# Loading scan operands earlier, computing the decay two units ahead, and wider queue reach in the ordering clock of a four-layer kernel

## The chip, the cores and the metric

The kernel runs on one core of a Trainium2 chip. The metric is the device time of one execution in microseconds (us), lower is better. The engines are TensorE (PE; its weight loads are PEld), VectorE (DVE), ScalarE (ACT) and GpSimd (POOL). SyncE (SP) issues DMAs; so do ACT and POOL.

## The reference

Four images of 96 x 64 x 64 pass a state-space scan (layer 0), a deformable convolution (layer 1), a Fourier layer with a feed-forward (2) and an attention with a feed-forward (3). The part that matters here is the scan, in four directions, 192 channels and 16 states:

```python
def step(h, inp):
    d_t, u_t, b_t, c_t = inp
    dA = jnp.exp(d_t[..., None] * A)
    h = dA * h + (d_t * u_t)[..., None] * b_t[:, :, None, :]
    y = jnp.einsum('bkdn,bkn->bkd', h, c_t)
    return (h, y)
...
_, ys = lax.scan(step, h0, (dl, ul, bl, cl))
```

## The kernel before

The scan is cut into 1536 *units* of 128 partitions (16 states x 8 channels) by 1024 pixels. Eight units make a *block* (64 channels), 24 a *step*. A unit runs: load `da` (ACT issues the DMA), `exp` on ACT, spread of `du` into PSUM on PE, multiply and scan on DVE, multiply by C on POOL, sum over states on PE, and once a block an eviction (`settle`) on ACT. The loop issues these stages skewed:

```python
for n in range(len(units) + 7):
    ...                                       # waits until layer 0 has made what unit n+4 needs
    for stage, m in ((self.inflow, n + 1), (self.decay, n + 1)):
        if at(m) is not None:
            stage(at(m))
    if n % 2 == 1 and at(n - 5) is not None:
        self.total(at(n - 5), at(n - 4))
    if loaded < len(units):
        self.fetch(units[loaded], units[loaded - 1])      # da of n+4; at a step start also bc,
        loaded += 1                                       # at a block start also du
    for stage, m in ((self.recur, n), (self.weigh, n - 2)):
        if at(m) is not None:
            stage(at(m))
    ...                                       # settle, store
    clock.unit(self.scanned[1])
    yield True                                # other layers' work is issued here
```

```python
def decay(self, u):                           # ACT
    u.decayed = self.net.clock.add(ACT, 1.15, 0.0)
    a = u.k * (DI // D8) + u.n
    self.net.nc.scalar.activation(u.da, u.da, AF.Exp, scale=self.al[:, a : a + 1])

def inflow(self, u):                          # PE, into one of two PSUM buffers
    u.spread = self.net.clock.add(PE, 1.1, self.scanned[1])
    db = self.ps.tile([128, 2, CH], F32, name=f"db{u.key}", tag="db", bufs=2)
    for h in range(2):
        self.net.nc.tensor.matmul(db[:, h, :], lhsT=self.rep[:96, u.s % 4, :],
            rhs=u.du[u.s // 4][:, h * CH : (h + 1) * CH], start=True, stop=True)
    ...
def recur(self, u):                           # DVE
    nc, clock = self.net.nc, self.net.clock
    clock.add(DVE, 1.22, u.spread)
    self.scanned = (self.scanned[1], clock.add(DVE, 2.33, u.decayed))
    nc.vector.tensor_mul(u.db, u.db, u.bc[:, 0, :])
    u.hh = self.sp.tile([128, T], F32, name=f"hh{u.key}", tag="hh", bufs=6)
    ...
    nc.vector.tensor_tensor_scan(u.along(u.hh), u.along(u.da), u.along(u.db), first, ALU.mult, ALU.add)
```

All other work is issued between units by two streams: `ends` (layer 0's inputs, then layers 2 and 3 image by image) and `middle` (layer 0's output, layer 1). In the traces an engine runs its instructions in the order in which they are issued (the change and fetch_late below, whose loads differ in time, show one and the same sequence of PE's 32696, DVE's 4484, ACT's 5798 and POOL's 4755 instructions), so the order is decided while the program is built, by a model *clock* that adds up estimated costs. It admits a step of work only if no engine that it uses is modelled further ahead of DVE than its *reach*:

```python
AHEAD = (2.0, 1.5, 3.0, 4.0)                  # reach of PE, DVE, ACT, POOL in us
PACE = 4.9
...
def has_room(self, work, ready):
    now = self.now()                          # max(ends[DVE], due); due grows by PACE a unit
    ...
    return all(not w or e <= now + a for w, e, a in zip(work, self.ends, AHEAD))
```

So AHEAD and the `clock.add` calls cost nothing on the chip; they only move instructions.

## Time and profile before

| | us |
|---|---|
| median of 3 runs | 9585 |
| first to last scan unit | 7799, that is 5.08 a unit |
| last scan unit to the end of layer 1's last sampling | 687 |
| rest of the third image | 245 |
| fourth image | 482 |

The stretches are read off the trace. The last three are called the *tail*. The chain of work that ended last is the view that says where the end came from (shares of the span, by engine and by line); before:

```profile
PE 29%; POOL 23%; DMA 16%; DVE 15%; issue 9%; ACT 6%; ACTq 1%; SPq 0%; DVEq 0%; POOLq 0%
POOL hh L904 11%; POOL g L1225 7%; DVE hh L895 7%; DMA da<-de 5%; PE pc L659 4%; DVE db L892 3%; PE ps L1248 3%; PE f L1339 3%; PE py L922 2%; PE po L1125 2%; PE db L879 2%; DMA du<-du 2%; DMA g<-table,idx 1%; ACT da L873 1%; POOL lw L747 1%
```

No engine carries a third of it, and loads carry 16%. Two groups of the page (count, then busy us and mean ns, then idle time of the engine just before them and what ended most of it):

```profile
L895 DVE TENSOR_TENSOR_SCAN hh<-da,st,db 128x1024 f32<-128x1024 f32 x1152 | 2703.1, 2346 | 494.9 <-ACT da L873 294.7
L873 ACT ACTIVATE da<-da,w_al 128x1024 f32<-128x1024 f32 x1536 | 1736.9, 1146 | 808.1 <-DMA da<-de 479.6
```

DVE waits before the scan, for the exp; ACT waits before the exp, for the load of `da`. It is tempting to read this as one cause. The experiments show that it is two.

### The profile page before, as it was taken

What the parts mean: (1) busy time and instruction counts of PE and PEld (TensorE: products, weight loads), DVE (VectorE), ACT (ScalarE), POOL (GpSimd) and SP (SyncE); (2) the same over time, 40 slices, a digit from 0 to 9 for tenths busy, and PEclk for the clock granted to TensorE, in tenths of its full rate; (3) what the DMA queues carried; (4) which work ended last, traced back from release to release, by engine and by line L of the source; (5) the groups of instructions that cost most, each with busy time, mean ns of one, the idle gap of its engine ahead of it and who ended that gap; (6) DMA issues with size and microseconds to landing.
All of it is one profiled execution on the core that took longest, in us unless ns stands there. A gap on an engine that the chain in (4) does not pass through costs nothing.

```text
span 9574.8 us, 93668 instructions
## 1 busy us (share of the span) xinstructions
PE 7024.3 (73%) x32684; PEld 3207.5 (33%) x32696; DVE 6758.3 (71%) x4516; ACT 4184.1 (44%) x5766; POOL 6460.4 (67%) x4755
## 2 busy tenths in 40 slices
PE   6675866696767667877666777777667787878887
PEld 2111311131222333212223444223334542377474
DVE  0378777877787888778877888888888789333313
ACT  3674666555544433555444233443333345311323
POOL 0585578666789998677899885667989657276101
PEclk9676977697877778877777888777778787889888
DMA  1476677766777877777777786767778777344010
GB/s 48 130 199 163 177 190 192 184 181 175 199 199 203 212 201 195 189 199 200 204 208 203 188 213 170 179 160 195 188 194 209 175 186 171 75 145 134 19 58 16
DMA packets 775821, 1609.55 MB, mean 168 GB/s; under 512 B 247665, under 2 KB 338829, under 8 KB 773238
## 3 DMA queue, kind: packets, MB, share of 16 engines
q10 hardware_dynamic: 300672, 985.79, 40.9%
q1 hardware_dynamic: 400950, 391.20, 15.0%
q0 software_dynamic: 73728, 226.57, 8.8%
q8 instruction: 260, 4.26, 0.2%
q14 instruction: 211, 1.73, 0.1%
HBM read 1346.94 MB, written 256.29 MB: 167 GB/s over the span
## 4 chain that ended last, share of the span: by engine, by line
PE 29%; POOL 23%; DMA 16%; DVE 15%; issue 9%; ACT 6%; ACTq 1%; SPq 0%; DVEq 0%; POOLq 0%
POOL hh L904 11%; POOL g L1225 7%; DVE hh L895 7%; DMA da<-de 5%; PE pc L659 4%; DVE db L892 3%; PE ps L1248 3%; PE f L1339 3%; PE py L922 2%; PE po L1125 2%; PE db L879 2%; DMA du<-du 2%; DMA g<-table,idx 1%; ACT da L873 1%; POOL lw L747 1%
## 5 line engine op out<-in xcount | busy, mean ns | idle before, releaser
L904 POOL TENSOR_TENSOR hh<-hh,bc 128x1024 f32<-128x1024 f32 x1536 | 3655.7, 2382 | 344.7 <-DVE hh L895 240.8
L895 DVE TENSOR_TENSOR_SCAN hh<-da,st,db 128x1024 f32<-128x1024 f32 x1152 | 2703.1, 2346 | 494.9 <-ACT da L873 294.7
L892 DVE TENSOR_TENSOR db<-db,bc 128x1024 f32<-128x1024 f32 x1536 | 1866.5, 1215 | 365.3 <-PE db L879 363.1
L873 ACT ACTIVATE da<-da,w_al 128x1024 f32<-128x1024 f32 x1536 | 1736.9, 1146 | 808.1 <-DMA da<-de 479.6
L879 PE MATMUL db<-du,rep 96*128 96x512 bf16 x3072 | 1120.5, 454 | 975.3 <-DVE hh L895 848.3
L1225 POOL DMA_INDIRECT g<-table,idx x1152 | 1429.9, 1241 | 397.8 <-issue 225.0
L922 PE MATMUL py<-hh,w_fold 128*32 128x512 f32 x6144 | 1153.0, 770 | 107.5 <-POOL hh L904 73.1
L895 DVE TENSOR_TENSOR_SCAN hh<-da,db 128x1024 f32<-128x1024 f32 x384 | 878.2, 2287 | 184.2 <-ACT da L873 131.1
L1248 PE MATMUL ps<-w_ident,g 128*96 128x128 f32 x4608 | 719.1, 321 | 365.8 <-DVE g L1234 159.3
L879 PEld LDWEIGHTS <-rep 96*128 96x128 bf16 x3072 | 275.0, 105 | 2036.8 <-issue 1250.7
L1234 DVE TENSOR_TENSOR g<-g,wt 128x3456 f32<-128x3456 f32 x128 | 544.6, 4255 | 408.1 <-DMA g<-table,idx 385.1
L1248 PEld LDWEIGHTS ps<-w_ident,g 128*96 128x96 f32 x4608 | 625.9, 151 | 560.3 <-issue 211.6
L902 POOL COPY st<-hh 128x1 f32<-128x1 f32 x1152 | 276.7, 240 | 793.0 <-DVE hh L895 753.6
L1256 ACT COPY st<-ps 96x384 f32<-96x384 f32 x384 | 182.5, 477 | 1245.5 <-PE ps L1248 1167.0
L746 POOL TENSOR_TENSOR w<-w,ex 128x512 f32<-128x512 f32 x192 | 246.9, 1286 | 565.2 <-ACT w L743 546.2
L659 PE MATMUL pc<-pad,wc 96*128 96x512 f32 x1152 | 545.1, 621 | 62.3 <-DMA wc<-wc_d 50.7
L1485 POOL CAST xqf<-fl 96x512 fp8e5<-96x512 f32 x64 | 55.0, 864 | 652.7 <-DVE fl L1443 617.8
L749 DVE SCALAR_TENSOR_TENSOR rl<-pd,lw 128x512 f32<-128x512 f32 x192 | 129.9, 677 | 397.1 <-POOL lw L747 396.0
L922 PEld LDWEIGHTS py<-hh,w_fold 128*32 128x32 f32 x6144 | 167.7, 123 | 676.0 <-issue 396.8
L768 PE MATMUL pr<-ex,w_ident 128*128 128x512 f32 x384 | 288.9, 843 | 83.7 <-POOL ex L758 39.4
L659 PEld LDWEIGHTS pc<-pad,wc 96*128 96x128 f32 x1152 | 223.4, 198 | 357.4 <-issue 328.3
L1426 DVE TENSOR_TENSOR t<-t,o 96x512 f32<-96x512 f32 x64 | 81.3, 1270 | 313.5 <-PE o L1424 313.4
(247 smaller groups left out, 9660.6 us busy)
## 6 DMA issues: line engine op xcount, KB each, us to landing
da<-de ACTq DMA_DIRECT2D x1536, 512.0 KB
du<-du ACTq DMA_DIRECT2D x384, 192.0 KB
bc<-bcd ACTq DMA_DIRECT2D x128, 512.0 KB
du<-du SPq DMA_DIRECT2D x128, 384.0 KB
y<-yb SPq DMA_DIRECT2D x384, 128.0 KB
de<-rl SPq DMA_DIRECT2D x128, 256.0 KB
m<-in_dft SPq DMA_DIRECT2D x128, 256.0 KB
du<-du SPq DMA_DIRECT2D x128, 192.0 KB
```

Source lines behind the costliest of these rows:

```text
L659: nc.tensor.matmul(pp, lhsT=wc[:, q, g * 128 : (g + 1) * 128], rhs=pad[:, r0 + dy : r0 + dy + NR, dx : dx + W], start=(q == 0), stop=(q == 8),
L768: nc.tensor.matmul(pr, lhsT=net.ident, rhs=ex, start=True, stop=False)
L873: self.net.nc.scalar.activation(u.da, u.da, AF.Exp, scale=self.al[:, a : a + 1])
L879: self.net.nc.tensor.matmul(db[:, h, :], lhsT=self.rep[:96, u.s % 4, :], rhs=u.du[u.s // 4][:, h * CH : (h + 1) * CH], start=True, stop=True,)
L892: nc.vector.tensor_mul(u.db, u.db, u.bc[:, 0, :])
L895: nc.vector.tensor_tensor_scan(u.along(u.hh), u.along(u.da), u.along(u.db), first, ALU.mult, ALU.add)
L904: self.net.nc.gpsimd.tensor_mul(u.hh, u.hh, u.bc[:, 1, :])
L922: nc.tensor.matmul(py[p0 : p0 + 32], lhsT=self.fold[:, u.i, :], rhs=hc[:, h * CH : (h + 1) * CH], start=u.sums["add"] is None and u.i == 0 ...
L1225: nc.gpsimd.indirect_dma_start(out=g[:, k, :], out_offset=None, in_=self.tables[b % 2], in_offset=bass.IndirectOffsetOnAxis(ap=idx[:, 9 * ...
L1234: nc.vector.tensor_mul(g4, g4, w4.unsqueeze(2).to_broadcast([128, 36, C]))
L1248: nc.tensor.matmul(pt[:, k, :], lhsT=g[:, k0 + k, c * C : (c + 1) * C], rhs=net.ident, is_transpose=True, start=(c == 0), stop=(c == 3),)
L1339: nc.tensor.matmul(pt[64 * part : 64 * part + 64, c, :], lhsT=d[:, :, c0 + c], rhs=matrix[:, 64 * part : 64 * part + 64], start=True, stop ...
```

## The change

It loads `bc` in the middle of the step before and `du` in the block before; takes the exp two units ahead of its scan (six `da` buffers, five loads ahead); gives the model clock longer reaches; and lets the clock know that a scan needs a free `hh` buffer and that a block's first sum needs the last one evicted. A narrower weight and shared tags make room in SBUF.

```diff
-AHEAD = (2.0, 1.5, 3.0, 4.0)
+AHEAD = (3.0, 3.0, 5.0, 7.0)
...
-        ahead = 4
+        ahead = 5
...
                 self.decay(at(0))
+                self.decay(at(1))
                 self.inflow(at(0))
-            for stage, m in ((self.inflow, n + 1), (self.decay, n + 1)):
+            for period, tick, load in ((24, 12, self.fetch_step), (8, 2, self.fetch_block)):
+                u = at(n - n % period + period)
+                if n % period == tick and u is not None and made(u):
+                    load(u)
+            for stage, m in ((self.inflow, n + 1), (self.decay, n + 2)):
...
+            if at(n) is not None:
+                self.recur(at(n), at(n - 6).summed if n >= 6 else 0.0)
...
-        u.da = sp.tile([128, T], F32, name=f"da{u.key}", tag="da", bufs=5)
+        u.da = sp.tile([128, T], F32, name=f"da{u.key}", tag="da", bufs=6)
...
-        self.scanned = (self.scanned[1], clock.add(DVE, 2.33, u.decayed))
+        self.scanned = (self.scanned[1], clock.add(DVE, 2.33, max(u.decayed, free)))
...
-        self.net.clock.add(PE, 1.5 + 1.3 * (u.i == 0), max(u.weighed, v.weighed))
+        ready = max(u.weighed, v.weighed, self.settled if u.i == 0 else 0.0)
+        u.summed = v.summed = self.net.clock.add(PE, 1.5 + 1.3 * (u.i == 0), ready)
...
-        self.net.clock.add(ACT, 0.6, 0.0)
+        self.settled = self.net.clock.add(ACT, 0.6, u.summed)
```

Cut: the split of `fetch` into three functions, the narrower weight, and the tags.

More of the change, by code (lines that the diff above doesn't have):

```diff
@@ L111, in prepare @@
     om = np.concatenate([ow[0::2], ow[1::2], w["L1_conv_mask_w"].reshape(9, C, 9)])
-    a["wom"] = wide(om.transpose(1, 2, 0))
+    a["wom"] = wide(om.transpose(1, 2, 0), 96)
     ob = w["L1_conv_offset_b"]
@@ L503, in __init__ @@
         self.ts = slice(self.j * T, (self.j + 1) * T)
+        self.bc = self.du = None
     def along(self, t):
@@ L558, in __init__ @@
         self.scanned = (0.0, 0.0)
+        self.settled = 0.0
     def before(self, b):
@@ L800, in at, with made @@
             return units[m] if 0 <= m < len(units) else None
+        def made(u):
+            return all(
+                (u.b, u.k, both, 2 * u.j + h) in self.ready for both in (False, True) for h in range(2)
+            )
         for n in range(len(units) + 7):
             for m in range(loaded, min(n + ahead + 1, len(units))):
-                u = units[m]
-                while not all(
-                    (u.b, u.k, both, 2 * u.j + h) in self.ready for both in (False, True) for h in range(2)
-                ):
+                while not made(units[m]):
                     yield False
@@ L822, in scan @@
                 loaded += 1
-            for stage, m in ((self.recur, n), (self.weigh, n - 2)):
-                if at(m) is not None:
-                    stage(at(m))
+            if at(n) is not None:
+                self.recur(at(n), at(n - 6).summed if n >= 6 else 0.0)
+            if at(n - 2) is not None:
+                self.weigh(at(n - 2))
             if n % 2 == 0 and at(n - 6) is not None and at(n - 6).i == 3:
@@ L839, in fetch @@
         halves = [slice(j * T + h * CH, j * T + (h + 1) * CH) for h in range(2)]
-        if u.first_of_step:
-            u.bc = sp.tile([128, 2, T], F32, name=f"bc{u.key}", tag="bc")
-            for s in range(2):
-                src = self.bc_d[b][k][NS * s : NS * s + NS, ts]
-                nc.scalar.dma_start(u.bc[:, s, :], src.unsqueeze(1).to_broadcast([NS, D8, T]))
-            if u.step == 0:
-                u.state = sp.tile([128, DI // D8], F32, name=f"st{u.key}", tag="st")
-            else:
-                u.state = before.state
-        else:
-            u.bc, u.state = before.bc, before.state
-        if u.first_of_block:
-            u.du = []
-            for q in range(2):
-                t = sp.tile([96, T], BF16, name=f"du{u.key}_{q}", tag=f"du{q}")
-                nc.scalar.dma_start(t, self.du_d[b][k][:, c0 + 32 * q : c0 + 32 * q + 32, ts])
-                u.du.append(t)
+        if not u.first_of_step:
+            u.bc = before.bc
+        elif u.bc is None:
+            self.fetch_step(u)
+        if u.first_of_step and u.step == 0:
+            u.state = sp.tile([128, DI // D8], F32, name=f"st{u.key}", tag="st")
+        else:
+            u.state = before.state
+        if not u.first_of_block:
+            u.du, u.sums = before.du, before.sums
+        else:
             u.sums = {"add": None}
-        else:
-            u.du, u.sums = before.du, before.sums
+            if u.du is None:
+                self.fetch_block(u)
         if u.i == 1 and u.s == 1 and (k == 0 or u.back):
@@ L865, in fetch, with fetch_step, fetch_block @@
         self.net.clock.add(ACT, 0.6, self.scanned[1])
-        u.da = sp.tile([128, T], F32, name=f"da{u.key}", tag="da", bufs=5)
+        u.da = sp.tile([128, T], F32, name=f"da{u.key}", tag="da", bufs=6)
         src = self.de_d[b][k][c0 + D8 * u.s : c0 + D8 * u.s + D8, ts]
         nc.scalar.dma_start(u.da, src.unsqueeze(0).to_broadcast([NS, D8, T]))
+    def fetch_step(self, u):
+        u.bc = self.sp.tile([128, 2, T], F32, name=f"bc{u.key}", tag="bc")
+        for s in range(2):
+            src = self.bc_d[u.b][u.k][NS * s : NS * s + NS, u.ts]
+            self.net.nc.scalar.dma_start(u.bc[:, s, :], src.unsqueeze(1).to_broadcast([NS, D8, T]))
+    def fetch_block(self, u):
+        u.du = []
+        for q in range(2):
+            t = self.sp.tile([96, T], BF16, name=f"du{u.key}_{q}", tag=f"du{q}")
+            c0 = 64 * u.g + 32 * q
+            self.net.nc.scalar.dma_start(t, self.du_d[u.b][u.k][:, c0 : c0 + 32, u.ts])
+            u.du.append(t)
     def decay(self, u):
@@ L886, in inflow, with recur @@
         u.db = db.rearrange("p h t -> p (h t)")
-    def recur(self, u):
+    def recur(self, u, free):
         nc, clock = self.net.nc, self.net.clock
         clock.add(DVE, 1.22, u.spread)
-        self.scanned = (self.scanned[1], clock.add(DVE, 2.33, u.decayed))
+        self.scanned = (self.scanned[1], clock.add(DVE, 2.33, max(u.decayed, free)))
         nc.vector.tensor_mul(u.db, u.db, u.bc[:, 0, :])
@@ L1015, in gated @@
                     cs = slice(j * CH, (j + 1) * CH)
-                    za = op.tile([128, CH], F32, name=f"za{b}_{j}", tag="za")
+                    za = op.tile([128, CH], F32, name=f"za{b}_{j}", tag="ya")
                     nc.sync.dma_start(za, self.z_d[b][:128, cs])
-                    zc = op.tile([D2, CH], F32, name=f"zc{b}_{j}", tag="zc")
+                    zc = op.tile([D2, CH], F32, name=f"zc{b}_{j}", tag="yc")
                     nc.sync.dma_start(zc, self.z_d[b][128:, cs])
@@ L1121, in chunk @@
                 r0 = j * NR
-                po = net.mm(f"po{b}_{j}")
+                po = net.mm(f"po{b}_{j}", 96)
                 for k in range(9):
```

## The prediction

> **What bounds the kernel now.** I read the page's busy shares first, then the busy time by stretch, then VectorE's (DVE) and ScalarE's (ACT) waits inside the long stretch, then the chain of work.
>
> The page's first part of the kernel before:
>
> ```profile
> PE 7024.3 (73%) x32684; PEld 3207.5 (33%) x32696; DVE 6758.3 (71%) x4516; ACT 4184.1 (44%) x5766; POOL 6460.4 (67%) x4755
> ```
>
> No engine is full on average. The busy time by stretch (columns: stretch, length, busy us and count of each engine, granted clock, DMA share, GB/s), cut where the 1536 units of the scan begin and end and where the last image's deformable layer and the third image end:
>
> ```profile
> 361.00:8161.00 7800.00, 5648.51 (x24317) 2310.58 (x24328) 6284.79 (x3946) 3641.66 (x4814) 5931.96 (x4325) 0.79 0.74 190
> 8174.00:8847.00 673.00, 549.55 (x3744) 409.58 (x3746) 224.70 (x203) 144.10 (x277) 402.52 (x325) 0.89 0.44 121
> 8847.00:9095.00 248.00, 201.38 (x1088) 117.35 (x1086) 92.60 (x128) 95.58 (x193) 43.25 (x34) 0.90 0.09 26
> 9095.00:9575.00 480.00, 391.21 (x3028) 276.96 (x3028) 131.35 (x189) 138.65 (x270) 41.59 (x34) 0.85 0.13 37
> ```
>
> Row one is the scan: 7800 us, 5.08 us a unit, and DVE, its nearest engine to a bound, is busy 6285 of them (81%). The other rows are a tail of 1414 us in which TensorE (PE) is busy 82% and no scan is left to hide anything. What DVE waits for in the scan:
>
> ```profile
> DVE hh L895 <- ACT da L873: 425.8, 212, 9.9
> DVE db L892 <- PE db L879: 363.1, 179, 16.4
> DVE g L1234 <- DMA g<-table,idx: 149.9, 44, 8.7
> DVE rl L749 <- POOL lw L747: 124.3, 54, 12.6
> DVE hh L895 <- PE py L922: 82.4, 61, 13.4
> ```
>
> (us in total, times, longest). 1 is the decay exp coming late from ACT, 2 the spread of du into PSUM late from PE, 5 an hh buffer not yet summed. What makes ACT late:
>
> ```profile
> ACT st L1256 <- PE ps L1248: 826.9, 241, 17.2
> ACT da L873 <- DMA da<-de: 479.6, 169, 16.6
> ...
> ACT yb L933 <- DMA du<-du: 123.9, 57, 20.6
> ```
>
> ACT runs in order, so an eviction waiting for PE holds the exp behind it, and a late load holds all. The chain through the second image's sampling (2780 to 3780 us) is another regime:
>
> ```profile
> by line: POOL hh L904 31.8%; POOL g L1225 25.0%; issue 8.9%; DMA g<-table,idx 4.3%; DVE hh L895 3.4%; POOL lw L747 3.1%; POOL w L746 2.8%; POOL st L902 2.6%; PE ps L1248 2.6%; DVE g L1234 2.4%; POOL ex L758 1.8%; DMA du<-du 1.7%; DVE db L89
> ```
>
> There GpSimd (POOL) carries the chain (92 to 94% busy in the trace, some 5.3 us a unit).
>
> **What the Trainium skill says.** "Perfetto Trace Analysis", Optimization Strategy, says that a kernel can have several regimes, that interleaving them may help, and to look for the gaps on the engine of interest and their semaphores. The trace agrees: three regimes (DVE starved, POOL-bound sampling, PE tail). "DMA: Bandwidth & Descriptors", Issuing engines are not separate DMA queues, says DMAs of all issuers share the same 16 engines and interleave; its Anatomy section gives a fit of 2 us plus bytes over 436 GB/s, so 3.2 us (an estimate) for a lone 512 KB da. Here pieces of 13 to 18 us of "DMA da" and "DMA du" stand in the chain, at a DMA share of 0.74: loads do not run alone, and bunching costs. The same section says DMA engines do not wait on semaphores, the issuing sequencer does; here that is ACT, and each issue takes it 0.53 us (da), 0.58 (bc), 0.74 (du).
>
> **The change part by part.**
>
> (1) Fetch of bc and du away from the step and block starts. Before, at a step start ACT issued 2 bc, 2 du and one da in a row, 2x0.58+2x0.74+0.53 = 3.2 us, and the da queued behind 1.4 MB. Grouping DVE's idle time before the two scan instructions by a unit's place in its step of 24 (from the trace) gives 124 us at place 0, 39 at 1, 66 at 14, 70 at 8, 47 at 16, 81 at 22, 59 at 23, and about 28 at an ordinary place. The excess over 28 at those seven is 290 us. The settle copy behind a du issue (the 123.9 us row) and the hh waits at places 14 and 22 belong to it. The issues are the same in number; I take 60% of it as removed: 175 us.
>
> (2) Decay two units ahead, sixth da buffer, loads five ahead. A load still has three units before its exp, so no DMA slack is won; the exp gains one more unit (5 us) before its scan. Of the 426 us, some 218 lie at the places counted in (1); of the other 208 (mean wait 2.0 us, longest 9.9) two thirds go: 140 us.
>
> Sum 315 us. But 555 of the 1536 units pass during sampling, where POOL sets the pace and DVE's saving is not time: 64% counts, 200 us.
>
> (3) Queue reach (2, 1.5, 3, 4) to (3, 3, 5, 7). This moves instructions, none are added. In the program order, by scan unit: sampling of images 0, 1, 2 takes 187, 165, 141 units against 197, 191, 167, so POOL's shared stretch is denser, 62 units fewer at 5.3 us and more at 4.9: some 25 to 50 us, I take 40. Image 1's last feed-forward, wholly in the tail before, ends inside the scan, and image 2's norm, first hidden layer and first DFT too. In the trace before that is 8174 to 8535, 360 us of the tail.
>
> The tail does not shrink by that. Image 3 must pass its deformable layer, which stands in the tail in both orders. Beside it PE gets about the same load from the other stream (summing that stream's matmul times, some 660 us before and 675 after), so its 673 us stay. But when it ends, image 2 has left only part of its attention and the last feed-forward (some 80 us of the trace's 9012 to 9095), against 248. The tail gets 248 - 80 = 165 us shorter; image 3's 480 us stay.
>
> What it costs: some 45 us of DVE work go into the scan, half of it into idle time (+25), and fuller PE queues ahead of the spread matmuls, which are still only one unit ahead, make the PE db wait grow by a tenth (+35).
>
> (4) The ordering clock now knows of hh buffers and settling; 96 columns for one weight and shared za/ya tags only make room in SBUF. No time of their own.
>
> **Sum:** scan -200 - 40 + 60 = -180; tail -165; together -345 from 9585: 9240 us, 3.6% faster.
>
> **Rivals.** (a) The PE spread becomes the wait. Two PSUM buffers tie it to the scan two units back, PE's reach grows by half, and the row is already 363 us. If it doubles, the scan gains nothing and only the tail's 165 us stay: about 9420, "same". Against it: PE is 72% busy in the scan, and the clock counts PE's delay before it admits more.
> (b) POOL queues seven us ahead hold the weighting back, hh buffers run out, and "hh <- PE py" grows from 82 us to several hundred in sampling: 9350 to 9450. Against it: the clock now waits for the hh buffer in its model, and sampling is POOL-bound already.
> (c) DMA becomes the bound: 0.74 share now, 0.78 at a scan 5% shorter, and da lands no earlier relative to its exp. Then decay two ahead is hidden anyway, and (2) is worth half: 9290.
> (d) It all lands: all 315 us count and denser sampling brings more; 9060 or lower.
>
> **Range and chances.** (d) and (a) set the range, 9060 to 9430. The 2% mark is 9394, 155 us above my number, close to where the scan gives nothing. I give 0.82 to faster, 0.15 to same, 0.03 to slower; slower needs both (a) and (b) at large size, with the tail gain surely there in the order.
>
> **What will show it right or wrong.** Step (1): the excess at places 0, 8, 22 and 23 and the row "yb <- DMA du" fall below half. Step (2): "hh <- ACT da" falls from 426 to under 150 us. Step (3): from the last scan to the end some 1250 us; image 2 ends about 80 us after the last sampling; sampling stretches busier than 94% on POOL. Costs: "db <- PE db" near 400 us. Scan near 7620 us, 4.96 a unit. The prediction is wrong if DVE's waits merely change name (DVE busy share in the scan stays 81%), or if the last deformable layer takes longer than 673 us because image 2 now competes harder.

## The result, and the profile after

The changed kernel took 9300 us (median of 4 runs, 9284 to 9337) against 9588 for the kernel before on the same chip (4 runs, 9584 to 9614): ratio 0.970, 95% interval 0.9666 to 0.9733. All runs were fast. A ratio here is the mean time of one kernel's fast runs over that of the other's fast runs of the same rounds, so not quite the ratio of the medians quoted.

The chain of work that ended last, after:

```profile
PE 28%; POOL 27%; DVE 17%; DMA 12%; issue 9%; ACT 6%; SPq 1%; ACTq 1%; DVEq 0%; another core or an unknown queue 0%; POOLq 0%
POOL hh L927 12%; POOL g L1249 9%; DVE hh L918 8%; PE pc L662 4%; DVE db L915 4%; PE py L946 3%; PE ps L1272 2%; PE f L1363 2%; PE db L901 2%; POOL lw L750 2%; POOL st L925 1%; DMA da<-de 1%; POOL w L749 1%; PE pd L1286 1%; PE po L1149 1%
```

Loads fell from 16% to 12% of the chain, `da` from 5% to 1%, and POOL and DVE took their place. The same two groups of the page, and the multiply's, after:

```profile
L918 DVE TENSOR_TENSOR_SCAN hh<-da,st,db 128x1024 f32<-128x1024 f32 x1152 | 2703.6, 2347 | 240.2 <-PE py L946 77.3
L895 ACT ACTIVATE da<-da,w_al 128x1024 f32<-128x1024 f32 x1536 | 1740.0, 1147 | 1178.0 <-DMA da<-de 504.7
L915 DVE TENSOR_TENSOR db<-db,bc 128x1024 f32<-128x1024 f32 x1536 | 1868.0, 1216 | 498.5 <-PE db L901 447.7
```

DVE's idle before the scan halved, although ACT's idle before the exp grew and its wait for `da` did not shrink (479.6 to 504.7 us). The load is as late as before; the exp simply has a unit more in hand. DVE's largest waits in the scan, after (us in total, times, longest):

```profile
DVE db L915 <- PE db L901: 447.7, 205, 26.8
DVE rl L752 <- POOL lw L750: 192.2, 99, 9.7
DVE g L1258 <- DMA g<-table,idx: 127.9, 40, 7.8
DVE hh L918 <- PE py L946: 89.3, 77, 6.1
DVE hh L918 <- ACT da L895: 31.8, 10, 11.8
```

The wait for the exp went from 425.8 to 31.8 us; that for the spread matmuls from 363.1 to 447.7. The busy time by stretch, after (stretch, length, busy us and count of PE, PEld, DVE, ACT, POOL, granted clock, DMA share, GB/s):

```profile
365.00:8016.00 7651.00, 5693.11 (x25030) 2341.99 (x25031) 6343.84 (x4003) 3705.93 (x4935) 5952.31 (x4341) 0.81 0.75 194
8016.00:8749.00 733.00, 601.02 (x3984) 459.41 (x3983) 209.32 (x186) 161.62 (x318) 406.15 (x326) 0.85 0.40 114
8749.00:8833.00 84.00, 68.72 (x208) 31.66 (x206) 38.20 (x58) 34.19 (x75) 18.96 (x17) 0.82 0.01 1
8833.00:9297.00 464.00, 373.16 (x3029) 265.79 (x3028) 133.39 (x189) 139.08 (x271) 42.64 (x34) 0.89 0.13 38
```

The scan took 7651 us against 7799 (-148) though DVE did 59 us more in it (6344 against 6285), and the tail 1281 against 1414 (-133). In the tail the third image's rest shrank from 245 to 84 us, but the stretch up to the last sampling grew from 687 to 733.

### The profile page after: what moved, and what is told of

It is laid out like the page before. It is cut to its first block, busy times and chain, and to the rows that moved or that the text cites. A ratio compares the mean times of both kernels' runs of the same rounds, so it can differ in the third digit from the quotient of the medians.

```text
span 9297.4 us, 93700 instructions
## 1 busy us (share of the span) xinstructions
PE 6961.3 (75%) x32696; PEld 3186.5 (34%) x32696; DVE 6749.8 (73%) x4484; ACT 4200.7 (45%) x5798; POOL 6459.2 (69%) x4755
## 4 chain that ended last, share of the span: by engine, by line
PE 28%; POOL 27%; DVE 17%; DMA 12%; issue 9%; ACT 6%; SPq 1%; ACTq 1%; DVEq 0%; another core or an unknown queue 0%; POOLq 0%
POOL hh L927 12%; POOL g L1249 9%; DVE hh L918 8%; PE pc L662 4%; DVE db L915 4%; PE py L946 3%; PE ps L1272 2%; PE f L1363 2%; PE db L901 2%; POOL lw L750 2%; POOL st L925 1%; DMA da<-de 1%; POOL w L749 1%; PE pd L1286 1%; PE po L1149 1%
## 5 line engine op out<-in xcount | busy, mean ns | idle before, releaser
L895 ACT ACTIVATE da<-da,w_al 128x1024 f32<-128x1024 f32 x1536 | 1740.0, 1147 | 1178.0 <-DMA da<-de 504.7
L915 DVE TENSOR_TENSOR db<-db,bc 128x1024 f32<-128x1024 f32 x1536 | 1868.0, 1216 | 498.5 <-PE db L901 447.7
L1249 POOL DMA_INDIRECT g<-table,idx x1152 | 1409.8, 1224 | 438.7 <-issue 239.6
L901 PE MATMUL db<-du,rep 96*128 96x512 bf16 x3072 | 1091.9, 444 | 736.2 <-DVE hh L918 679.8
L925 POOL COPY st<-hh 128x1 f32<-128x1 f32 x1152 | 300.3, 261 | 637.3 <-DVE hh L918 591.8
L1372 ACT COPY d<-f 128x512 f32<-128x512 f32 x192 | 112.4, 585 | 446.5 <-PE f L1363 336.6
```

The lines of the kernel that those rows point to most:

```text
L925: self.net.nc.gpsimd.tensor_copy(u.state[:, u.n : u.n + 1], u.hh[:, last : last + 1])
L1249: nc.gpsimd.indirect_dma_start(out=g[:, k, :], out_offset=None, in_=self.tables[b % 2], in_offset=bass.IndirectOffsetOnAxis(ap=idx[:, 9 * ...
```

## The experiments

Twelve kernels, all correct, all runs fast, each three rounds, on three chips; every ratio is to the kernel before on the same chip. Scan, tail and waits are from each kernel's one trace. As the chips differ a little, compare two runs by their ratios, or by the stretches of their traces. The tail is split as above: to the last sampling + rest of the third image + fourth image. "exp" and "spread" are DVE's waits in the scan for ACT's exp and PE's spread matmuls, in us.

| run | ratio to before (95%) | scan | tail | exp | spread |
|---|---|---|---|---|---|
| before | 1 | 7799 | 1414 = 687+245+482 | 426 | 363 |
| the change | 0.9700 (0.9666 to 0.9733) | 7651 | 1281 = 733+84+464 | 32 | 448 |
| reach_back | 0.9788 (0.9764 to 0.9813) | 7588 | 1392 = 668+259+465 | 45 | 374 |
| reach_only | 0.9796 (0.9773 to 0.9820) | 7798 | 1199 = 702+29+468 | 515 | 354 |
| decay_one | 0.9761 (0.9740 to 0.9782) | 7696 | 1278 = 707+103+468 | 451 | 356 |
| decay_only | 0.9775 (0.9747 to 0.9803) | 7679 | 1295 = 685+134+476 | 40 | 450 |
| fetch_late | 0.9811 (0.9793 to 0.9829) | 7738 | 1264 = 705+83+476 | 54 | 542 |
| fetch_only | 0.9936 (0.9915 to 0.9957) | 7672 | 1467 = 721+266+480 | 433 | 307 |
| clock_blind | 0.9686 (0.9662 to 0.9710) | 7619 | 1266 = 723+78+465 | 22 | 466 |
| pe_reach_back | 0.9807 (0.9775 to 0.9838) | 7629 | 1366 = 726+178+462 | 49 | 403 |
| pe_reach_alone | 0.9853 (0.9820 to 0.9886) | 7670 | 1370 = 692+216+462 | 39 | 387 |
| pool_reach_back | 0.9720 (0.9698 to 0.9741) | 7700 | 1250 = 733+49+468 | 55 | 458 |
| blind_pe4 | 0.9769 (0.9746 to 0.9792) | 7798 | 1172 = 685+20+467 | 49 | 627 |
| blind_pace52 | 0.9934 (0.9913 to 0.9956) | 7999 | 1135 = 664+0+471 | 22 | 589 |

### reach_back: the change without its reach

```diff
-AHEAD = (3.0, 3.0, 5.0, 7.0)
+AHEAD = (2.0, 1.5, 3.0, 4.0)
```

> The changed kernel with the queue reach alone set back to (2, 1.5, 3, 4). In its program order the work after the last scan unit is as in the kernel before (five feed-forward layers and two whole Fourier layers; the changed kernel has four and less than two). Theory A (the reach buys the tail and costs the scan a little): the tail is as long as before, some 1410 us against 1281, the scan is shorter than the changed kernel's 7651 us by 20 to 60 us because the wait of the scan's multiply for the spread matmuls falls back from 448 to about 370 us; time 9350 to 9400 us. Rival B (the reach is also what shortens the scan, by keeping other engines fed): scan back near 7750 us, time about 9500 us.

Ratio 0.9788 (9350 us): theory A. The tail is 1392 us, near the old one, and the scan is the shortest of all, 7588 us. The stretches of this run (tail first, the scan last):

```profile
7952.00:8620.00 668.00, 538.36 (x3634) 398.82 (x3632) 220.30 (x204) 147.75 (x292) 404.45 (x326) 0.89 0.44 122
8620.00:8879.00 259.00, 214.84 (x1289) 130.48 (x1286) 90.42 (x127) 98.61 (x198) 41.10 (x34) 0.90 0.08 25
8879.00:9344.00 465.00, 375.22 (x3031) 265.86 (x3029) 133.55 (x189) 139.17 (x271) 43.62 (x34) 0.89 0.13 38
363.00:7952.00 7589.00, 5552.60 (x24301) 2285.79 (x24299) 6308.60 (x3946) 3648.94 (x4807) 5933.30 (x4325) 0.80 0.76 195
```

Fetch, decay and clock together take 211 us out of the scan; putting the reach on top gives 63 of them back and takes 111 from the tail. The spread wait is 374 us without the reach and 448 with it.

### reach_only: the kernel before with the reach alone

```diff
-AHEAD = (2.0, 1.5, 3.0, 4.0)
+AHEAD = (3.0, 3.0, 5.0, 7.0)
```

> The kernel before with the queue reach alone set to (3, 3, 5, 7). In its program order the work left when the last sampling ends is a little less than the changed kernel's (the third image's attention is past). Theory A (the reach buys the tail, some 135 us, and costs the scan by fuller queues): time 9420 to 9520 us, scan 7780 to 7880 us with the waits for the exp and for the spread matmuls both larger than before (426 and 363 us). Rival B (reach alone is worth the whole 280 us): about 9300 us.

Ratio 0.9796 (9358 us), between the two theories: A said 9420 or more, B about 9300. The scan stayed at 7798 us although it took in more work, and the tail fell by 215 us to 1199. DVE's waits in this run's scan:

```profile
DVE hh L895 <- ACT da L873: 514.7, 238, 13.7
DVE db L892 <- PE db L879: 354.1, 175, 16.4
```

So A's place was right (tail, not scan) and its cost was wrong: here the extra work filled time in which DVE idled anyway (1514 us of idle in the scan before, 1480 here). Reach alone is worth 2.0%, the rest alone (reach_back) 2.1%, and both 3.0%; had they multiplied, the ratio would be 0.959. That fits two gains that draw on the same idle time of DVE, but was not isolated.

### decay_one: the change with the exp one unit ahead

```diff
                 self.decay(at(0))
-                self.decay(at(1))
                 self.inflow(at(0))
...
-            for stage, m in ((self.inflow, n + 1), (self.decay, n + 2)):
+            for stage, m in ((self.inflow, n + 1), (self.decay, n + 1)):
```

> The changed kernel with the exp one unit ahead instead of two (six da buffers and five loads ahead kept, so a load now has four units instead of three before its exp). Theory A (it is the exp's second unit that hides late loads and late evictions): the wait of the scan for the exp comes back from 32 us to 200 to 400 us, the scan is 100 to 200 us longer, time 9400 to 9480 us. Rival B (the loads' place is what matters; with early fetches and a load four units ahead the exp is on time anyway): the wait stays under 100 us, time within 50 us of the changed kernel's 9300.

Ratio 0.9761, 0.6% slower than the change. What DVE waits for in the scan, and ACT's wait for `da`, in this run:

```profile
DVE hh L917 <- ACT da L894: 451.0, 225, 13.6
DVE db L914 <- PE db L900: 356.2, 147, 17.8
ACT da L894 <- DMA da<-de: 138.0, 35, 17.6
```

The exp wait came back in full, as theory A said, although each load had four units before its exp and ACT's wait for loads fell to 138 us. So late loads were not what made the exp late at DVE: with them mostly gone the exp is just as late. What is left is ACT's own queue, and the traces tell what stood in it. Take, for each late exp, the time by which it was late, counted back from its start. In the kernel before (426 us in all) ACT was executing other instructions for 289 us of it, was issuing DMAs or waiting before such an issue for 95, and waited for the exp's own load for 39. In this run (451 us) it was 298, 149 and 7. An earlier wait, whose backlog ACT then works off, is not excluded.

The time was less than A asked (9335, not 9400 to 9480). As the exp wait rose by 419 us, DVE's other waits fell: that for the spread by 92, that for GpSimd's `lw` by 103, that for `hh` by 44, and many small ones. In sum DVE's idle in the scan rose only from 1307 to 1366 us.

### decay_only: the kernel before with the exp two units ahead alone

The edit is `ahead = 5`, six `da` buffers, `self.decay(at(1))` at the start, `(self.decay, n + 2)` in the loop, and the edits that make room.

> The kernel before with the exp two units ahead alone (loads five ahead, six da buffers, and the three edits that make room for them). Its program order leaves less after the scan than before's (four feed-forward layers against five). Theory A (the exp's second unit is worth what the prediction said, 140 us of VectorE's wait of which two thirds are time): VectorE's wait for the exp falls from 426 us to under 100, the spread wait rises since late du and the step starts remain, scan 7650 to 7720 us, 0.985 to 0.990 of before with the tail's part. Rival B (with fetch alone at 0.6% and the three together at 3.0%, the exp's second unit carries most of what is left): 0.980 or less.

Ratio 0.9775: rival B's "0.980 or less". Exp wait 40 us, spread wait up to 450, scan 7679 as A had it. But the tail fell too, to 1295, because an exp that the clock counts a unit earlier changes which work it admits: the order left four feed-forward layers after the scan instead of five. Its 2.2% is therefore about half scan, half order, and cannot be set against one wait. Why the clock admits more then was not followed up.

### fetch_late: the change with bc and du loaded late

```diff
-                if n % period == tick and u is not None and made(u):
+                if False and n % period == tick and u is not None and made(u):
```

> The changed kernel with bc and du fetched as in the kernel before, with the step's or block's first da; all compute engines' orders are the same as in the changed kernel. Theory A, after the traces (the early fetch only moves the queueing of da from the units at places 0, 8 and 16 of a step to 7, 15 and 23, and the exp's second unit hides it in both places): time within 40 us of 9300, ScalarE's wait for da about 500 us. The prediction's step 1 (bunched loads cost 175 us of VectorE's idle, some 110 us of time): 9400 us or more, with VectorE's waits at places 0 and 8 back to 120 and 70 us, from late du for the spread matmuls, which stay one unit ahead.

Ratio 0.9811, 1.1% slower than the change. By the ratios that is about 105 us, the prediction's size and not theory A's; the time itself, 9373 us, lies between A's 9340 and the other's 9400, and the two traces differ by 64 us (scan 86 longer, tail 17 shorter). The order of PE, DVE, ACT and POOL is that of the changed kernel, so nothing but the loads' place differs. DVE's and ACT's waits in the scan:

```profile
DVE db L915 <- PE db L901: 542.3, 230, 27.6
DVE hh L918 <- ACT da L895: 54.1, 21, 8.4
ACT da L895 <- DMA da<-de: 449.6, 157, 17.6
```

The loss is in the spread wait (448 to 542 us). Grouping DVE's idle before the unit's two instructions by place in the step gives 53 us at place 0 in the changed kernel and 111 here.

Theory A was right about `da`, which the totals hide. By place, ACT's wait for `da` stands at 0, 8 and 16 here (236 of its 450 us) and at 7, 15 and 23 in the changed kernel (256 of 505). The early loads only move this queueing, and the exp's second unit hides it in both.

So the gain is on PE's side. It is tempting to say that `du` now arrives in time for the spread matmuls, but the traces are against it. What PE waited for in the scan, first in the changed kernel, then here (L768 and L773 are ACT's copies in layer 0's input stream):

```profile
PE pr L775 <- ACT du L773: 83.9, 59, 6.3
PE pr L772 <- ACT du L768: 47.0, 32, 9.7
PE db L901 <- DMA du<-du: 3.7, 1, 3.7
```

```profile
PE pr L775 <- ACT du L773: 134.2, 65, 12.5
PE pr L772 <- ACT du L768: 75.6, 36, 18.6
PE db L901 <- DMA du<-du: 18.6, 9, 4.6
```

The wait for `du` grew by 15 us, and after none of its nine waits did DVE have to wait for the spread of that unit. All waits of PE for ACT together grew from 309 to 389 us. ACT is the engine that issues these loads, so they most likely hold up its other work, for which PE then waits in front of the spread; that way is argued, not isolated.

### fetch_only: the kernel before with the early loads alone

The edit is the `for period, tick, load` loop with its two functions (and the narrower weight and shared tags), on the old `ahead`, `decay`, clock and reach.

> The kernel before with the early fetch of bc and du alone; every compute engine's order is the same as before. Theory A (the early fetch is worth what its undoing cost, 1.1%): time 0.985 to 0.992 of before, all of it in the scan (7690 to 7730 us against 7799), the tail 1400 to 1420 us; VectorE's idle at place 0 of a step falls from 124 to about 60 us. Rival B (it pays only together with the exp's second unit, because the da behind an early du is late at places 7, 15 and 23 instead): 0.995 to 1.0, VectorE's idle rises at places 7, 15 and 23.

Ratio 0.9936: between the two theories. By the traces A's place holds: the scan fell by 127 us to 7672, place 0's idle from 124 to 48 us (55 of these 76 us were waits for the exp), and PE's wait for `du` before the spread, in the whole trace, from the first line below (before) to the second (this run):

```profile
PE db L879 <- DMA du<-du: 101.9, 31, 14.5
```

```profile
PE db L900 <- DMA du<-du: 22.9, 5, 14.4
```

Again this wait is not itself the gain: of the 31 before, only the first, at the start of the program, was followed by more than 0.6 us of DVE waiting in front of that unit's multiply. PE's waits for ACT in the scan fell from 485 to 362 us. The exp wait as a whole did not fall (426 to 433 us): at place 13, whose exp comes right behind the new issue of `bc` in ACT's queue, DVE's idle rose from 27 to 84 us, 67 of it for the exp. In the change, with the exp two units ahead, place 13 has 24 us.

But the tail, with the same order of instructions, took 53 us more, 1467. The stretches of that tail:

```profile
8035.00:8756.00 721.00, 588.42 (x3816) 427.66 (x3818) 224.86 (x204) 146.32 (x291) 403.36 (x326) 0.86 0.40 113
8756.00:9022.00 266.00, 222.33 (x1079) 129.37 (x1078) 90.05 (x126) 94.97 (x192) 40.84 (x34) 0.79 0.08 25
9022.00:9502.00 480.00, 390.11 (x3031) 275.72 (x3029) 133.64 (x190) 138.87 (x271) 43.87 (x34) 0.84 0.12 37
```

The granted TensorE clock is 0.86 and 0.79 where the kernel before had 0.89 and 0.90. PE's busy time times the clock is the same work: 588 x 0.86 + 222 x 0.79 = 682 here, 560 x 0.89 + 200 x 0.90 = 679 before (687 and 246 us stretches cut at 8160, 8847 and 9093). The fourth image bears this product out: it is 329 to 336 in all 14 traces, at clocks from 0.84 to 0.91. So in this one trace part of the scan's gain was lost to the clock of the tail. What sets that clock was not tested.

### clock_blind: the change without the clock's new waits

```diff
-                self.recur(at(n), at(n - 6).summed if n >= 6 else 0.0)
+                self.recur(at(n), 0.0)
...
-        ready = max(u.weighed, v.weighed, self.settled if u.i == 0 else 0.0)
+        ready = max(u.weighed, v.weighed)
...
-        self.settled = self.net.clock.add(ACT, 0.6, u.summed)
+        self.settled = self.net.clock.add(ACT, 0.6, 0.0)
```

> The changed kernel with the ordering clock blind again to hh buffers and to settling. In its program order the second stream stands slightly further at the end of the scan (200 of the second Fourier matmuls left against 256). Theory A (no time of its own): 0.965 to 0.973 of before. Rival B (the clock's new waits hold other work back, and are why reach and fetch plus decay, 2.0% and 2.1% apart, give only 3.0% together): 0.958 to 0.963.

Ratio 0.9686: theory A. Its interval overlaps the change's, and the two ran on different chips, so it is not shown to be faster. The clock's better knowledge is not what the reach and the rest lose when joined.

### pe_reach_back, pe_reach_alone and pool_reach_back: which engine's reach

```diff
-AHEAD = (3.0, 3.0, 5.0, 7.0)
+AHEAD = (2.0, 3.0, 5.0, 7.0)     # pe_reach_back
+AHEAD = (3.0, 1.5, 3.0, 4.0)     # pe_reach_alone
+AHEAD = (3.0, 3.0, 5.0, 4.0)     # pool_reach_back
```

> The changed kernel with TensorE's reach alone back at 2.0. In its program order image 1's feed-forward is not finished at the end of the scan (414 of its matmuls left against 384) and the third image's Fourier is not begun. Theory A (TensorE's reach buys the tail and costs the wait for the spread matmuls): that wait falls from 448 to about 370 us, the scan from 7652 to 7590 to 7620 us, the tail grows from 1281 to 1330 to 1380 us; time 9290 to 9340 us at the changed kernel's 9300. Rival B (the spread wait is a matter of chance in the order, not of reach): wait above 420 us, scan as long, time 9360 or more.

> The changed kernel with the reach of VectorE, ScalarE and GpSimd back at 1.5, 3 and 4 and TensorE's left at 3. In its program order five feed-forward layers are left after the scan, as in the kernel before, and 216 of the last Fourier matmuls after the last sampling (changed kernel 144). Theory A (TensorE's reach only admits work together with the others', as a step of work needs room on all its engines): 0.975 to 0.980, near the 0.979 of no reach at all, tail above 1330 us. Rival B (TensorE's reach is the whole worth of the reach, since taking it away alone gave 0.981): 0.967 to 0.972.

> The changed kernel with GpSimd's reach alone back at 4.0. In its program order the second stream stands as far as in the changed kernel at the end of the scan, and further when the last sampling ends (66 of the attention's matmuls left against 115). Theory A (GpSimd's reach buys nothing, as sampling is GpSimd-bound with or without it): time 0.965 to 0.972 of before, image 2's rest after the last sampling 30 to 60 us. Rival B (it is what makes sampling denser and so the scan shorter): scan 30 us longer or more, 0.974 or more.

Taking PE's reach away gave 0.9807, no better than no reach at all (0.9788): theory A had the direction of every number (spread wait 403, scan 7629, tail 1366) but set the scan's gain against the tail's loss evenly; it was 22 us against 85, and the time, 9367 us, is the one that B named (9360 or more). Leaving PE's alone gave 0.9853, worse than A's 0.975 to 0.980 and nowhere near B's 0.967 to 0.972. So neither half works without the other, as a step of work needs room on every engine it uses. GpSimd's reach can go: 0.9720, theory A, within the change's interval, though the scan grew by 48 us, as rival B had it, while the tail shrank by 31. Whether DVE's or ACT's is PE's needed partner was not run. Nor was a second order at one and the same reach: each setting gives one order of instructions, so a part of such differences can be the luck of the order.

### blind_pe4 and blind_pace52: two candidates beyond the change

```diff
+AHEAD = (4.0, 3.0, 5.0, 7.0)     # blind_pe4, on clock_blind
...
+PACE = 5.2                       # blind_pace52, on clock_blind with AHEAD as in the change
```

> A second candidate: the clock blind, and TensorE's reach 4.0 in place of 3.0. In its program order image 2 is past its attention at the end of the last sampling (66 matmuls left, before the fourth image's own 66: none of its own), and sampling of the second and third images takes 141 and 116 scan units. Theory A (more reach keeps buying tail and the spread wait pays for it): tail 1190 to 1230 us, the spread wait 500 us or more, scan 7640 to 7700 us, 0.965 to 0.971, level with the blind clock's 0.969. Rival B (the spread wait stays near 450 us): 0.960 to 0.964.

> A candidate beyond the change: the clock blind again (0.969 of before) and its pace of a unit 5.2 us in place of 4.9, so that more other work is admitted to each unit. In its program order the third image is nearly through at the end of the scan (288 feed-forward matmuls left, that is three layers) and nothing but the fourth image is left after the last sampling. Theory A (work moved out of the tail gains as long as the tail is longer than the last deformable layer plus the fourth image): tail 1080 to 1150 us against 1266, scan longer by 50 to 120 us than 7620, 0.962 to 0.972. Rival B (the scan has no idle left to take it): scan longer by over 150 us, 0.975 or more.

Both moved work out of the tail as said, or further, and lost more than that in the scan. One more us of PE reach: tail 1172 instead of 1266, scan 7798 instead of 7619, ratio 0.9769, worse than either theory. The spread wait in clock_blind and in blind_pe4:

```profile
DVE db L915 <- PE db L901: 465.7, 191, 20.8
```

```profile
DVE db L915 <- PE db L901: 626.5, 246, 21.6
```

A unit's pace of 5.2: tail 1135, scan 7999, ratio 0.9934, its rival B. No version run here is shown to beat the change.

## Why the prediction was right

It said 9240 us in a range of 9060 to 9430; measured 9300. It asked for 180 us from the scan and 165 from the tail; the traces show 148 and 133. (It counts images from 0: its images 2 and 3 are the third and the fourth.) Taking its steps one by one:

- **Scan, steps (1) and (2): -200 us.** reach_back has both, with the clock and without the reach: 7799 to 7588, -211. Right in sum, which is in part luck: its shares of 60% and two thirds were guesses, and step (1)'s reason was half wrong. By the ratios, undone one at a time they are worth 1.1% (fetch_late, some 105 us; predicted 64% of 175, that is 112) and 0.6% (decay_one, some 60 us; predicted 64% of 140, that is 90).
- **Step (1)'s reason was half wrong.** It put the loss down to `da` queued behind the bunch. That queueing is there: 312 of ACT's 480 us of waits for `da` stood at places 0, 8 and 16. But the early loads moved it (505 us after, 256 of them at 7, 15 and 23), and what they gained went with PE's waits for ACT (fetch_late, fetch_only), which the step does not name. Its signs came: the excess at places 0, 8, 22 and 23 fell from 222 to 49 us and the row "yb <- DMA du" from 123.9 to 15.0, but that row is as good as gone in fetch_late (0) and decay_only (3.9) too, where the loads are late. The excess at its seven places halved, from 290 to 146 us, but place 14 rose from 66 to 119; that place stays at 46 to 97 in the other runs of early loads with a different order, so it most likely belongs to this order.
- **Step (2)'s sign of success came:** exp wait below 150 us (32). It also said that no DMA slack is won, which ACT's wait for `da` bears out. decay_one adds that loads were not the main cause. One reading was off: the 218 us that it leaves to step (1) lack places 14 and 22; with all seven it is 247, which leaves 179, and two thirds of that are 120 us, not 140. Two smaller ones: pieces of "DMA da" in the chain reach 19.7 us, not 18, and GpSimd's 92 to 94% holds inside sampling, not for the whole of it (2758 of 3011 us, 92%).
- **Step (3), tail: -165 us; measured -133.** The third image's rest after the last sampling was 84 us, predicted 80. The miss is "its 673 us stay": the stretch to the last sampling grew by 46 us (687 to 733). A longer last deformable layer, by competition of its image 2, was one of its own two signs of being wrong, and this one came. PE's busy time times granted clock in it is 499 before and 511 after, so some 14 us (12 over 0.85) are more work, about the difference of its 660 and 675 us; the rest goes with a clock of 0.85 instead of 0.89, which it did not consider. The fourth image shortened by 18 us at 0.89 instead of 0.85. (The other sign, DVE's share in the scan staying at 81%, did not come: 83%.)
- **Step (3), cost to the scan: +60, with 40 gained from denser sampling, so +20; measured +63** (7588 to 7651). The 40 us are the mis-sized term. Set against reach_back, sampling (from the first to the last gather of the first three images) took 255 us less, 2769 for 3024, but 506 units passed in it for 578, so that a unit there took 5.47 us for 5.23. The other 72 units, at 4.74 us each outside sampling, cost 341 us. So the denser sampling gained nothing, and POOL's busy share in it stayed at 91 to 92% (2758 of 3011 us before, 2529 of 2769 after) where 94% was named as its sign. The spread wait rose by 74 us on top of reach_back, where 35 were allowed, but 67 of them lie outside sampling (238 to 305 us), where a unit took no longer (4.76 us without the reach).
- **Step (4), the clock: no time of its own.** clock_blind agrees within the intervals.
- **Rival (a)**, the spread matmul as the new wait, did not come at a reach of 3: the wait grew from 363 to 448 us, far from double. At 4 (blind_pe4) it reached 627, and the scan lost more than the tail returned. Rival (b), GpSimd's reach starving `hh`, did not happen: 82.4 to 89.3 us. Rival (c) did not either: DMA share 0.74 and 0.75.

What the prediction lacked was the overlap of its own parts. It gave the reach one gain and one cost, whatever else the change does. Reach alone costs the scan nothing and takes 215 us from the tail; on top of the rest it costs 63 and takes 111.

## What to carry to other kernels

When an engine waits for A and A waits for B, do not assume that B is the cause: here giving the middle instruction one unit more lead removed the wait at the end while the load stayed as late, and giving the load more lead in place of that did not. Group a wait by its place in the loop before you say that it stayed: an unchanged total hid that the wait for `da` had moved. In a kernel whose issue order decides how work interleaves, a wider queue reach can be free in one version and cost time in the next, as here on top of the other fixes, so tune it last and together with them. Split the time into its stretches for every run, and read the granted clock of a matmul-bound stretch before explaining a difference of a few per cent in it.

## What the Trainium skill lacked or had wrong

- "TensorE: Matmul & The Clock Gate", Part 1, says that the length of the clock's ramp varies from run to run and that, for modelling, it costs below 1% of a typical kernel's span. It has no figure for how far one and the same PE-bound stretch varies, where the clock weighs more. The fourth image, the same instructions in every kernel, took 462 us at a granted clock of 0.90 to 0.91, 464 to 469 at 0.88 to 0.89, and 476 to 482 at 0.84 to 0.86 (blind_pace52 is left out, as its fourth image starts beside the last sampling). These 20 us are 0.2% of the kernel, but 4% of the stretch. Each is one trace, and what sets the clock was not tested.
- "Perfetto Trace Analysis", Optimization Strategy, says to find the gaps on the engine of interest and the instruction that ends the wait. It does not say that the next link back may be another matter: ACT's wait for loads fell from 505 to 138 us in decay_one while DVE's wait for ACT rose from 32 to 451.
- "DMA: Bandwidth & Descriptors", Anatomy of one DMA: the fit that the prediction names was measured on DMAs issued from GpSimd. The page has none for those issued from ACT, as `da` is, so the prediction's estimate from it is cut. The page has the sharing of engines by all issuers, but no figure for what a load then waits: ACT's waits for 512 KB loads in the changed kernel last up to 17.7 us at a mean DMA share of 0.75.
